# A graph-attention kernel: other superblock sizes at the end, a divided last quad, and ones written by ScalarE

## Chip, cores and metric

One NeuronCore of a Trainium2 chip runs the kernel. The metric is device time in microseconds (us) of one execution; of several runs the median is taken. The kernel before takes 2886.38 us (median of 5 runs, 2878.96 to 2889.55).

## What is computed

A graph with 12500 nodes and 200000 edges, sorted by destination. Each node's row `x` (128 numbers) is normalized and clipped at zero, and multiplied by a weight matrix; each edge gets an attention logit per head (4 heads) from its source, its destination and its 64 edge features. A softmax over all edges of one destination weighs the source rows, and the sum is added to `x`:

```python
h = jnp.maximum(_layernorm(x), 0.0)
h = (h @ W_node.T).reshape(N, H, HD)
e = (edge_attr_64 @ W_edge.T).reshape(E, H, HD)
att = jnp.sum(jnp.concatenate([h[src], h[tgt], e], -1) * a, axis=-1)
att = jnp.where(att > 0, att, 0.2 * att)
m = jnp.maximum(segment_max(att, tgt), 0.0)
ex = jnp.exp(att - m[tgt])
denom = segment_sum(ex, tgt) + (E - deg)[:, None] * jnp.exp(-m)
out = x + segment_sum((ex / denom[tgt])[:, :, None] * h[src], tgt)
```

## The kernel before

**Node part (lines 330 to 411).** A table of 137 numbers for each node is computed and written to device memory: four heads of 32 values with a one behind each, a further one for counting edges (column `R_CNT`), and four source logits (`R_SRC`).

**Edges.** They are cut into 392 groups of 511 edges (512 places); four groups are a *quad* (98 quads, numbered 0 to 97). GpSimd gathers the table rows of a quad's edges into a tile `ga` with 16 indirect DMAs (`gather`, line 135), 14 for the last quad. There are eight `ga` buffers, so the gather of quad q + 8 waits until quad q has been summed. The first four quads are gathered from `x`, before the table exists, and are turned into table rows on the chip by `converted` (lines 235 to 266): transposes and matmuls on TensorE, copies by ScalarE (line 261), and at the end of each quad two memsets by VectorE (lines 263 and 265) that put the ones in place. `late(q)` (line 709) runs it.

**Group loop (lines 775 to 807).** The quads are bundled in *superblocks*: 2 and 2 quads, then twenty-two of 4, then 2, 2, 1 and 1 (`ends`, line 426; 28 superblocks). For each quad there are two kinds of work, and for each superblock one:

- `logits(q)` (line 490): VectorE compares (line 497), TensorE multiplies (502, 505), and `add_sources` (517, 519) closes the quad. Opening a quad's logits also issues, on SyncE, the loads for the quad two ahead.
- `softmax(s)` (line 530): one chain across TensorE, VectorE and ScalarE for a whole superblock, from the transposes (544) through `low` (546), the scans (553, 575, 578, 581) and the exponential (587) to the copies `facs` (605) and `xs` (610).
- `sums(q)` (line 646): for each group, VectorE scales the gathered rows (663) and makes a one-hot matrix (666), and TensorE sums by matmul (671). `complete_group` (627) finishes the group before: VectorE carries the last row over (632), TensorE adds it (637), ScalarE copies the result to `pt` (638). After the fourth group ScalarE makes `den` (642), and one `complete` later VectorE divides the quad in six instructions (`divide`, 681 to 692). SyncE then stores the quad's four windows of `out` (694).

The order on every engine is that of the program: `together` takes one step of each of its generators in turn. The last quad of superblock s - 1 is summed together with the softmax of s and with the first logits of superblock s + 1; the other quads of s are summed together with further logits of s + 1, as long as there are any. So in this kernel a step of the loop is the sums of one quad with the logits of a later quad or without them, and with a softmax or without one.

Of the kernel before, what the change touches and what calls it, by code (L numbers as in the profile page):

```python
# [11 lines left out]
AF = mybir.ActivationFunctionType  # L12
OP = mybir.AluOpType
AX = mybir.AxisListType

P = 128
H, HD = 4, 32
HW = HD + 1
D = H * HD
# [5 lines left out]
R_CNT, R_SRC, ROW = H * HW, H * HW + 1, H * HW + 5  # L25

J = 4
GE = J * P
NE = GE - 1
WIN = 96  # L30
# [10 lines left out]
def blocks(total, step):  # L41
    return [(i, min(step, total - i)) for i in range(0, total, step)]
# [3 lines left out]
def kernel(  # L46
# [35 lines left out]
    nc = tc.nc  # L82
# [21 lines left out]
    ones = consts.tile([P, P], F32, name="ones")  # L104
# [13 lines left out]
    quads = blocks(G, QG)  # L118
    nq = len(quads)
# [26 lines left out]
    with tc.manual_schedule():  # L146
# [88 lines left out]
        def converted(q, psum, turn_pool, copy):  # L235

            ga = GA[q]
            m = quads[q][1]
            made = []

            def turned_over(i):
                hT_ps = psum.tile([P, 512], F32, name="acc")
                hT_ps = hT_ps.rearrange("p (j e) -> p j e", j=J)
                for j in range(J):
                    nc.tensor.transpose(hT_ps[:, j, :], ga[:, i, j, 0:D], ident)
                hT = turn_pool.tile([P, J, P], F32, name="hT_e", bufs=2)
                copy(hT, hT_ps)
                made.append(hT)

            turned_over(0)  # L250
            for i in range(m):
                yield
                if i + 1 < m:
                    turned_over(i + 1)
                for k in range(J // 2):
                    row_ps = psum.tile([P, 512], F32, name="acc")
                    row_ps = row_ps.rearrange("p (j e) -> p j e", j=2)
                    for j in range(2):
                        nc.tensor.matmul(row_ps[:, j, :ROW], made[i][:, 2 * k + j, :],
                                         wcat, start=True, stop=True)  # L260
                    nc.scalar.copy(ga[:, i, 2 * k:2 * k + 2, :], row_ps[:, :, :ROW])
            rows = ga[:, :m].rearrange("p g j r -> p (g j) r")
            nc.vector.memset(
                rows[:, :, 0:H * HW].rearrange("p t (h w) -> p t h w", w=HW)[:, :, :, HD], 1.0)
            nc.vector.memset(rows[:, :, R_CNT:R_CNT + 1], 1.0)
            yield


# [16 lines left out]
        with tc.tile_pool(name="node", bufs=2) as node, tc.tile_pool(  # L285
# [48 lines left out]
            ends = [3, 6]  # L334
# [88 lines left out]
    per = SBG // QG  # L423


    ends = [2, 2], [2, 2, 1, 1]
    amid = max(nq - sum(ends[0]) - sum(ends[1]), 0)
    supers = []
    for m in ends[0] + [n for _, n in blocks(amid, per)] + ends[1]:
# [5 lines left out]
    with tc.tile_pool(name="work", bufs=2) as work, \  # L435
            tc.tile_pool(name="turned", bufs=1) as turned, \
            tc.tile_pool(name="ps", bufs=1, space=bass.MemoryType.PSUM) as ps:
        XW, LG, AT, U, DR = {}, {}, {}, {}, {}
# [4 lines left out]
        share_ps = const_ps[0:WIN, WIN + G:].rearrange("p (g h) -> p g h", h=H)  # L443
# [10 lines left out]
        def window(g):  # L454
            return nc.values_load(
                base[0:1, g:g + 1], engines=[mybir.EngineType.SP], min_val=0, max_val=N - 1,
                skip_runtime_bounds_check_because="a destination, which is a node")
# [159 lines left out]
        state = {}  # L617

        def complete():

            division = state.pop("division", None)
            if begun:
                complete_group(*begun.pop())
            if division:
                divide(*division)

        def complete_group(q, i, ga, hot, pt, acc, fc):
            g0, m = quads[q]
            g = g0 + i
            if g:  # L630
                before = state["before"]
                nc.vector.tensor_tensor(  # L632
                    ga[0:1, i, 0, 0:H * HW].rearrange("p (h w) -> p h w", w=HW),
                    before[WIN:WIN + 1, 0:H * HW].rearrange("p (h w) -> p h w", w=HW),
                    fc.unsqueeze(2).to_broadcast([1, H, HW]), op=OP.mult)
                nc.scalar.copy(ga[0:1, i, 0, R_CNT:R_CNT + 1], before[WIN:WIN + 1, R_CNT:R_CNT + 1])  # L636
            nc.tensor.matmul(acc, hot[:, i, 0, :], ga[:, i, 0, :], start=False, stop=True)  # L637
            nc.scalar.copy(pt[:, i, :], acc)  # L638
            state["before"] = pt[:, i, :]
            if i == m - 1:  # L640
                den = work.tile([WIN, QG, H], F32, name="den")
                nc.scalar.activation(den[:, :m, :], pt[0:WIN, :m, R_SRC:R_SRC + H], AF.Exp,
                                     scale=-1.0)
                state["division"] = q, pt, den

        def sums(q):

# [25 lines left out]
                begun.append((q, i, ga, hot, pt, acc, fc[:, :, g - s0]))  # L673
                yield

        def divide(q, pt, den):

            g0, m = quads[q]
            xw = XW.pop(q)
            others = work.tile([WIN, QG], F32, name="others")  # L680
            nc.vector.tensor_scalar(others[:, :m], pt[0:WIN, :m, R_CNT], -1.0, float(E),
                                    op0=OP.mult, op1=OP.add)
            nc.vector.tensor_tensor(den[:, :m, :], den[:, :m, :],
                                    others[:, :m].unsqueeze(2).to_broadcast([WIN, m, H]), op=OP.mult)
            val = pt[0:WIN, :m, 0:H * HW].rearrange("p g (h w) -> p g h w", w=HW)
            nc.vector.tensor_tensor(den[:, :m, :], den[:, :m, :], val[:, :, :, HD], op=OP.add)
            nc.vector.reciprocal(share_ps[:, :m, :], den[:, :m, :])
            res = work.tile([WIN, QG, D], F32, name="res")
            nc.vector.tensor_tensor(  # L689
                res[:, :m, :].rearrange("p g (h d) -> p g h d", d=HD), val[:, :, :, 0:HD],  # L690
                share_ps[:, :m, :].unsqueeze(3).to_broadcast([WIN, m, H, HD]), op=OP.mult)
            nc.vector.tensor_tensor(res[:, :m, :], res[:, :m, :], xw[:, :m, 0:D], op=OP.add)  # L692
            for i in range(m):
                nc.sync.dma_start(out[bass.ds(window(g0 + i), WIN), :], res[:, i, :])

        def all_logits(q):
            flush()
# [11 lines left out]
        def late(q, copy=nc.scalar.copy):  # L709

            return [converted(q, acc_pool, work, copy)]
# [276 lines left out]
```

## Time and profile before

| what | value |
|---|---|
| median of 5 runs | 2886.38 us |
| the profiled execution's own time | 2883.8 us |
| its span, first to last instruction | 2881.9 us |
| TensorE matmul / VectorE / ScalarE / GpSimd busy | 48% / 47% / 15% / 52% of the span |
| mean granted TensorE clock | 0.522 |
| first gathers | 161 us |
| quad 0 summed (`den`, line 642) | 301.78 us |
| quad 97 summed | 2867.14 us |
| last store issued | 2876.27 us |

"Busy" counts computing instructions; waiting instructions and the issue of DMAs are not counted. In the rows of the profile, `out<-in` are tiles by the program's names, `x4` is a number of instructions, and the bracket of a timeline row gives the engine's idle time before it and what ended that. "issue" means that the profile shows nothing that was waited for, and "remote" that a semaphore was raised by something that the profile cannot name. One core runs here, so "remote" is no other core.

### The profile page before, as it was taken

The page shows a single profiled execution, that of the slowest core. Times are in us where ns is not written, and L with a number is a line of the kernel's source. Part 1 is how long each engine was busy: PE and PEld are TensorE (multiplying, and loading weights), DVE is VectorE, ACT ScalarE, POOL GpSimd, SP SyncE. Part 2 cuts the span into 40 slices and gives each one's busy share as a digit, 9 for nine tenths or more (in the row PEclk, how much of TensorE's full clock was granted, in tenths as well). Part 3 has the DMA queues.
Part 4 walks back from the last instruction along what each step waited for, and adds up shares of the span by engine and source line. Part 5 has one row for each costly group of instructions (what it writes and reads, how often), then busy time and mean ns, then how long its engine had stood idle before and what let it go on. Part 6 is the DMA issues. An engine that isn't in the chain of part 4 may idle for free.

```text
span 2881.9 us, 29033 instructions
## 1 busy us (share of the span) xinstructions
PE 1396.6 (48%) x7275; PEld 1253.9 (44%) x7275; DVE 1363.6 (47%) x3314; ACT 428.0 (15%) x1766; POOL 1491.8 (52%) x1574
## 2 busy tenths in 40 slices
PE   2524655445445455454454454454454454454465
PEld 1424644444444444444344444354454444444364
DVE  2523454444444454454454454354454454454376
ACT  1524201111111111111111111111111111111121
POOL 7152345555555555555556556555556555556510
PEclk6765555555555555555555555555555555555555
DMA  4333344343344344344344344344444343444320
GB/s 141 119 108 79 94 126 116 93 112 105 101 111 108 103 115 109 91 125 106 100 109 110 102 111 108 101 109 101 110 111 110 101 112 101 107 111 109 84 69 15
DMA packets 214493, 299.10 MB, mean 104 GB/s; under 512 B 86121, under 2 KB 162153, under 8 KB 204914
## 3 DMA queue, kind: packets, MB, share of 16 engines
q1 hardware_dynamic: 162512, 184.97, 23.2%
q0 software_dynamic: 50112, 109.65, 15.7%
q10 hardware_dynamic: 1698, 2.58, 0.3%
q8 instruction: 61, 1.00, 0.1%
q14 instruction: 110, 0.90, 0.1%
HBM read 270.49 MB, written 26.52 MB: 103 GB/s over the span
## 4 chain that ended last, share of the span: by engine, by line
another core or an unknown queue 23%; PE 15%; DVE 10%; issue 7%; ACT 2%; DMA 0%; SPq 0%; ACTq 0%; DVEq 0%
PE acc L671 8%; PE lg L505 3%; PE acc L637 2%; DVE at L497 2%; ACT pt L638 1%; DVE res L692 1%; DVE res L689 1%; DVE run L575 1%; DVE ga L632 1%; PE lg L502 1%; DVE hot L666 1%; DVE ga L663 1%; DVE run L553 0%; DVE top L581 0%
## 5 line engine op out<-in xcount | busy, mean ns | idle before, releaser
L135 POOL DMA_INDIRECT ga<-table,srci x1502 | 1430.1, 952 | 1241.2 <-PE acc L637 719.8
L671 PE MATMUL acc<-ga,hot 128*97 128x137 f32 x2352 | 650.6, 448 | 755.9 <-ACT ga L659 520.8
L671 PEld LDWEIGHTS acc<-ga,hot 128*97 128x97 f32 x2352 | 518.7, 279 | 782.5 <-ACT ga L659 530.1
L632 DVE TENSOR_TENSOR ga<-pt,facs 1x132 f32<-1x132 f32 x391 | 112.5, 288 | 1027.0 <-ACT pt L638 703.3
L638 ACT COPY pt<-acc 97x137 f32<-97x137 f32 x392 | 107.4, 274 | 2052.0 <-remote 1248.9
L505 PE MATMUL lg<-wblk,ea 128*128 128x8 f32 x1568 | 409.1, 359 | 0.0
L505 PEld LDWEIGHTS lg<-wblk,ea 128*128 128x128 f32 x1568 | 381.7, 309 | 0.0
L637 PE MATMUL acc<-ga,hot 128*97 128x137 f32 x784 | 263.0, 439 | 162.5 <-issue 76.1
L502 PEld LDWEIGHTS <-at 96*128 96x128 bf16 x1568 | 213.4, 165 | 226.8 <-DVE at L497 130.2
L663 DVE TENSOR_TENSOR ga<-ga,ex_ps 128x528 f32<-128x528 f32 x392 | 270.3, 690 | 8.6 <-PE ex_ps L598 8.2
L637 PEld LDWEIGHTS acc<-ga,hot 128*97 128x97 f32 x784 | 195.9, 282 | 178.2 <-issue 84.2
L497 DVE TENSOR_TENSOR at<-const_ps,db 96x512 bf16<-96x512 f32 x392 | 266.9, 682 | 7.4 <-DMA db<-in_dst_dram 1.5
L502 PE MATMUL lg<-pw,at 96*128 96x12 bf16 x1568 | 169.3, 181 | 154.5 <-DVE at L497 106.8
L666 DVE TENSOR_TENSOR hot<-const_ps,slot 128x384 f32<-128x384 f32 x392 | 213.8, 545 | 0.0
L598 PE MATMUL ex_ps<-ident,ex 64*128 64x64 f32 (+2 forms) x112 | 18.6, 314 | 212.1 <-ACT ex L587 212.1
L598 PEld LDWEIGHTS ex_ps<-ident,ex 64*128 64x128 f32 (+2 forms) x112 | 13.8, 208 | 215.1 <-ACT ex L587 215.1
L372 PE MATMUL row_ps<-wcat,hT 128*128 128x137 f32 x198 | 41.5, 362 | 83.7 <-DVE hT L364 24.9
L636 ACT COPY ga<-pt 1x1 f32<-1x1 f32 x391 | 73.9, 189 | 10.6
L372 PEld LDWEIGHTS row_ps<-wcat,hT 128*128 128x128 f32 x198 | 35.2, 254 | 90.0 <-issue 45.8
L135 POOL DMA_INDIRECT ga<-in_x_dram,srci x64 | 60.7, 948 | 20.7 <-issue 19.2
L692 DVE TENSOR_TENSOR res<-res,xw 96x512 f32<-96x512 f32 x98 | 67.8, 692 | 3.4
L689 DVE TENSOR_TENSOR res<-pt,const_ps 96x512 f32<-96x512 f32 x98 | 66.9, 683 | 3.4
(129 smaller groups left out, 1013.2 us busy)
## 6 DMA issues: line engine op xcount, KB each, us to landing
db<-in_dst_dram SPq DMA_DIRECT2D x98, 768.0 KB
ea<-in_edge_t_dram SPq DMA_DIRECT2D x98, 512.0 KB
ga<-table,srci POOLq DMA_INDIRECT x1502
xw<-in_x_dram SPq DMA_DIRECT2D x392, 48.0 KB
out_dram<-res SPq DMA_DIRECT2D x392, 48.0 KB
pw<-side SPq DMA_DIRECT2D x392, 2.2 KB
table<-row SPq DMA_DIRECT2D x9, 616.5 KB
xt<-in_x_dram SPq DMA_DIRECT2D x9, 576.0 KB
```

The source lines that it names most:

```text
L135: nc.gpsimd.indirect_dma_start(out=ga[:, i, j, 0:width], out_offset=None, in_=rows, in_offset=bass.IndirectOffsetOnAxis(ap=srci[:, g0 + i, ...
L497: nc.vector.tensor_tensor(at[:, i, :], node_ps[0:WIN, g0 + i:g0 + i + 1].to_broadcast([WIN, GE]), db[:, i, :], op=OP.is_equal)
L502: nc.tensor.matmul(lg[:, i, j].rearrange("p k h -> p (k h)"), at[:, i, j * P:(j + 1) * P], sw, start=i + j == 0, stop=False, skip_group_ch ...
L505: nc.tensor.matmul(lg[:, i, 2 * w:2 * w + 2, 0, :], ea[:, i, w, :], wblk, start=False, stop=True, skip_group_check=True)
L632: nc.vector.tensor_tensor(ga[0:1, i, 0, 0:H * HW].rearrange("p (h w) -> p h w", w=HW), before[WIN:WIN + 1, 0:H * HW].rearrange("p (h w) -> ...
L637: nc.tensor.matmul(acc, hot[:, i, 0, :], ga[:, i, 0, :], start=False, stop=True)
L638: nc.scalar.copy(pt[:, i, :], acc)
L663: nc.vector.tensor_tensor(val, val, heads(ex)[:, :, :, g - s0].unsqueeze(3).to_broadcast([P, J, H, HW]), op=OP.mult)
L666: nc.vector.tensor_tensor(hot[:, i, :, 0:WIN], lane_ps.unsqueeze(1).to_broadcast([P, J, WIN]), slot[:, g, :].unsqueeze(2).to_broadcast([P, ...
L671: nc.tensor.matmul(acc, hot[:, i, j, :], ga[:, i, j, :], start=j == 1, stop=False)
L689: nc.vector.tensor_tensor(res[:, :m, :].rearrange("p g (h d) -> p g h d", d=HD), val[:, :, :, 0:HD], share_ps[:, :m, :].unsqueeze(3).to_br ...
L692: nc.vector.tensor_tensor(res[:, :m, :], res[:, :m, :], xw[:, :m, 0:D], op=OP.add)
```

## The change

There are three edits.

1. The ones of the converted quads 0 to 3 are written by ScalarE, as two copies from a tile of ones, in place of the two memsets on VectorE.
2. The last superblocks have 3, 3, 2, 2, 2, 2 quads in place of 2, 2, 1, 1. The number of 4-quad superblocks falls from 22 to 20; there are 28 superblocks as before. Of the last 16 quads, those summed together with a softmax are 83, 86, 89, 91, 93 and 95, where they were 83, 87, 91, 93, 95 and 96; those summed without logits of a later quad are 82, 88, 95, 96 and 97, where they were 89, 90, 94, 96 and 97.
3. The last quad is divided and stored group by group: four times six VectorE instructions on one group each, and `den` is made four times by ScalarE.

TensorE, GpSimd and SyncE keep the number of their instructions. VectorE gets 18 more and loses 8, and handles smaller softmaxes at the end; ScalarE gets 11 more (8 copies and 3 `den`). The loop's waits in the 4-quad superblocks are the same as before.

```diff
             rows = ga[:, :m].rearrange("p g j r -> p (g j) r")
-            nc.vector.memset(
-                rows[:, :, 0:H * HW].rearrange("p t (h w) -> p t h w", w=HW)[:, :, :, HD], 1.0)
-            nc.vector.memset(rows[:, :, R_CNT:R_CNT + 1], 1.0)
+            nc.scalar.copy(
+                rows[:, :, 0:H * HW].rearrange("p t (h w) -> p t h w", w=HW)[:, :, :, HD],
+                ones[:, 0:1].unsqueeze(2).to_broadcast([P, m * J, H]))
+            nc.scalar.copy(rows[:, :, R_CNT], ones[:, 0:m * J])
...
-    ends = [2, 2], [2, 2, 1, 1]
+    ends = [2, 2], [3, 3, 2, 2, 2, 2]
...
-            if i == m - 1:
+            if i == m - 1 or q == nq - 1:
+                lo = i if q == nq - 1 else 0
                 den = work.tile([WIN, QG, H], F32, name="den")
-                nc.scalar.activation(den[:, :m, :], pt[0:WIN, :m, R_SRC:R_SRC + H], AF.Exp,
-                                     scale=-1.0)
-                state["division"] = q, pt, den
+                nc.scalar.activation(den[:, lo:i + 1, :], pt[0:WIN, lo:i + 1, R_SRC:R_SRC + H],
+                                     AF.Exp, scale=-1.0)
+                state["division"] = q, pt, den, lo, i + 1
...
-        def divide(q, pt, den):
+        def divide(q, pt, den, lo, hi):
+            n = hi - lo
+            xw = XW[q][:, lo:hi]
+            pt = pt[0:WIN, lo:hi]
+            den = den[:, lo:hi]
...
-            for i in range(m):
-                nc.sync.dma_start(out[bass.ds(window(g0 + i), WIN), :], res[:, i, :])
+            for i in range(n):
+                nc.sync.dma_start(out[bass.ds(window(quads[q][0] + lo + i), WIN), :], res[:, i, :])
```

More of the change, by code (lines that the diff above doesn't have):

```diff
@@ L674, in sums @@
                 yield
-        def divide(q, pt, den):
-            g0, m = quads[q]
-            xw = XW.pop(q)
+        def divide(q, pt, den, lo, hi):
[3 more added lines that the diff above has]
+            den = den[:, lo:hi]
             others = work.tile([WIN, QG], F32, name="others")
-            nc.vector.tensor_scalar(others[:, :m], pt[0:WIN, :m, R_CNT], -1.0, float(E),
+            nc.vector.tensor_scalar(others[:, :n], pt[:, :, R_CNT], -1.0, float(E),
                                     op0=OP.mult, op1=OP.add)
[L683 to L687, printed above, removed]
+            nc.vector.tensor_tensor(den, den, others[:, :n].unsqueeze(2).to_broadcast([WIN, n, H]),
+                                    op=OP.mult)
+            val = pt[:, :, 0:H * HW].rearrange("p g (h w) -> p g h w", w=HW)
+            nc.vector.tensor_tensor(den, den, val[:, :, :, HD], op=OP.add)
+            nc.vector.reciprocal(share_ps[:, :n, :], den)
             res = work.tile([WIN, QG, D], F32, name="res")
             nc.vector.tensor_tensor(
-                res[:, :m, :].rearrange("p g (h d) -> p g h d", d=HD), val[:, :, :, 0:HD],
-                share_ps[:, :m, :].unsqueeze(3).to_broadcast([WIN, m, H, HD]), op=OP.mult)
-            nc.vector.tensor_tensor(res[:, :m, :], res[:, :m, :], xw[:, :m, 0:D], op=OP.add)
-            for i in range(m):
-                nc.sync.dma_start(out[bass.ds(window(g0 + i), WIN), :], res[:, i, :])
+                res[:, :n, :].rearrange("p g (h d) -> p g h d", d=HD), val[:, :, :, 0:HD],
+                share_ps[:, :n, :].unsqueeze(3).to_broadcast([WIN, n, H, HD]), op=OP.mult)
+            nc.vector.tensor_tensor(res[:, :n, :], res[:, :n, :], xw, op=OP.add)
+            for i in range(n):
+                nc.sync.dma_start(out[bass.ds(window(quads[q][0] + lo + i), WIN), :], res[:, i, :])
         def all_logits(q):
```

## The prediction

> **What bounds the kernel now.** I read the busy shares first (no engine is over 52%, so none is simply full), then the waits, then the timelines of GpSimd and ScalarE against each other. Rows of the waits (engine, line, releaser: total us, times, longest):
>
> ```profile
> ACT pt L638 <- remote: 1248.9, 105, 18.9
> POOL ga L135 <- PE acc L637: 719.8, 86, 61.0
> ...
> DVE ga L263 <- issue: 39.8, 2, 21.1
> ```
>
> ScalarE waits about once in each of 98 quads, 1248.9 / 105 = 11.9 us each, for a sum that TensorE finished issuing long before; GpSimd waits for the last matmul of a quad (line 637), which frees a buffer. GpSimd's timeline:
>
> ```profile
> 2714.05 0.94 POOL L135 DMA_INDIRECT ga<-table,srci  x1 [5.12 <-PE acc L637]
> ...
> 2732.97 0.95 POOL L135 DMA_INDIRECT ga<-table,srci  x1 [0.30 <-issue]
> 2736.86 0.95 POOL L135 DMA_INDIRECT ga<-table,srci  x1 [2.94 <-remote]
> ```
>
> A batch of 16 gathers takes 2733.92 - 2714.05 = 19.9 us and starts when a quad is summed. The ends of quads, from ScalarE's timeline:
>
> ```profile
> 1501.52 0.22 ACT L642 ACTIVATE den<-pt 96x16 f32<-96x16 f32 x1
> 1524.67 0.22 ACT L642 ACTIVATE den<-pt 96x16 f32<-96x16 f32 x1
> 1550.56 0.22 ACT L642 ACTIVATE den<-pt 96x16 f32<-96x16 f32 x1
> 1576.30 0.22 ACT L642 ACTIVATE den<-pt 96x16 f32<-96x16 f32 x1
> 1608.66 0.22 ACT L642 ACTIVATE den<-pt 96x16 f32<-96x16 f32 x1
> ...
> 2776.74 0.22 ACT L642 ACTIVATE den<-pt 96x16 f32<-96x16 f32 x1
> 2789.51 0.22 ACT L642 ACTIVATE den<-pt 96x16 f32<-96x16 f32 x1
> 2809.75 0.22 ACT L642 ACTIVATE den<-pt 96x16 f32<-96x16 f32 x1
> 2820.46 0.22 ACT L642 ACTIVATE den<-pt 96x16 f32<-96x16 f32 x1
> 2840.14 0.22 ACT L642 ACTIVATE den<-pt 96x16 f32<-96x16 f32 x1
> 2857.81 0.22 ACT L642 ACTIVATE den<-pt 96x16 f32<-96x16 f32 x1
> 2867.14 0.22 ACT L642 ACTIVATE den<-pt 96x16 f32<-96x16 f32 x1
> ```
>
> While gathers run, a step with logits takes 25.8 us (1550.56 to 1576.30), one with a softmax too 32.4. After the last gather (2754.2) a step with logits takes 12.8 (2776.74 to 2789.51), with softmax and logits 20.2, with a softmax alone 17.7, of sums alone 9.3 to 10.7. So a gather batch holds the engines up: some 7 us of a step's work gets done beside its 20 us, the rest comes after it, and only then is the next buffer free. GpSimd and the compute engines take turns. The change leaves that loop alone from quad 4 to 81; it acts on three places at its ends.
>
> **Place 1, the ones (first edit).** VectorE's timeline:
>
> ```profile
> 260.86 0.17 DVE L201 SCALAR_TENSOR_TENSOR shift<-both,rstd 128x16 f32<-128x16 f32 x1
> 264.18 0.11 DVE L263 MEMSET ga<- 128x64 f32 x1 [3.14 <-ACT ga L261]
> ...
> 319.19 0.11 DVE L263 MEMSET ga<- 128x64 f32 x1 [18.68 <-issue]
> ...
> 323.04 0.27 DVE L519 TENSOR_TENSOR U<-st,ga 128x64 f32<-128x64 f32 x1
> 326.57 0.69 DVE L549 TENSOR_TENSOR t_ps<-t_ps,low 32x511 f32<-32x511 f32 x1
> ```
>
> The memset costs 0.11 us but waits for ScalarE's last copy, and everything behind it on VectorE waits too. Its four instances:
> - Quad 0 (236.5): behind it stands a copy that TensorE's transposes release only at 247.2. Nothing gained; ScalarE's two copies sit before row scalings that end 7 us earlier. 0.
> - Quad 1 (264.18): behind it stand 10 us of ready work (lines 517, 519, 497, 186), back to back until 271.0; ScalarE then waits for it (`rstd`, 271.04, idle 3.1 us). Without the memset VectorE goes on at 261.07 and is through at 267.9. ScalarE's own queue ends at 267.9 plus 0.4 for the two copies, so `rstd` moves from 271.04 to 268.3: **-2.7**.
> - Quad 2 (286.9): VectorE waited only 0.4 us; ScalarE is the late one (`facs` starts right as its scalings end, 287.83), so the two copies count: **+0.5**.
> - Quad 3 (319.19): TensorE and ScalarE convert until 318.67 + 0.39. VectorE can do lines 663, 666, the division of quad 0 and 517 meanwhile (3.3 us); `U` (519) needs the converted rows, so it moves from 323.04 to about 319.6. Next late is TensorE: sums (1.7 us), logits (1.1), transposes (0.9) from 319.8, then `low` 0.6: line 549 moves from 326.57 to about 324.1: **-2.4**.
>
> A ScalarE copy of these shapes isn't in the trace. From below: 0.12 us, the spacing of the 128x16 copies at line 659; from above: 0.39 us, line 261 with 128x274. I take 0.2 to 0.25, near 659's own 0.21. All eight on the path would cost 1 to 3 us. Sum -4.6; bounds -7 (3.14 and 3.9 gained in full) and +2 (the gathers of 301.7 to 321.2 still hold TensorE, and the copies cost).
>
> [...]
>
> **Place 2, the superblocks (second edit).** Number and kind of all work stay; only which step holds which changes.
> - Under gathers (quads 82 to 90): two steps with logits become a softmax step and the step after it. In the trace twenty 4-quad superblocks average 108.4 us (for example 1501.52 to 1608.66 is 107.1) against 4 x 25.8 = 103.1, so a softmax costs **+5.3** here, the following step giving back some 1.3 of 6.6. Two steps of sums alone stay two, 22.8 us each (last gather end + 2.7); the one with the short batch of 14 keeps its 2.5 us advantage.
> - After the gathers (91 to 97): softmax+logits three times, logits once, softmax once and sums twice before; now softmax+logits twice, logits twice, the rest alike: 12.8 - 20.0 = **-7.2**. A sums-only step after a softmax-only one took 9.3, another 10.7: I add 0.4.
>
> Sum **-1.5**; bounds -5 (the softmax is hidden under the batch as far as 7 us of compute are) and +4 (6.6 paid each time, sums 2 us dearer).
>
> **Place 3, the last quad (third edit).** Now: last `pt` at 2867.1, six divisions 2.4 us, then four stores, each waiting for the one before: 2869.55, 2872.16, 2874.75, 2876.27; the end follows 5.6 us later. A group's division, for which no row exists, is bounded by 2.4 (the whole quad) and 1.0 (six of the 0.17 us rows); from 0.17, 0.17, 0.18, 0.26 and two of 0.29 (1x132, line 632) with gaps I take 1.6. Divisions 0 and 1 stand before lines 663 and 632 on VectorE, so the last `pt` comes 1.6 us later, 2868.7; the last division ends at about 2870.9. The stores of quad 96 were issued from 2860.55 at 1.52 us spacing, the fourth at 2865.09; four more behind them at this spacing go at 2866.6, 2868.1, 2869.7 and 2871.2. Last store 5.1 us earlier; of its 7 gaps some will be slower (the median of this wait is 1.55, a tenth exceed 2.25, two of the last three were 2.60), so I take **-4.2**, bounds -5.5 and +2.5 (all at 2.60: 2860.55 + 18.2 = 2878.75). `res` has two buffers, so division 1 waits for quad 96's stores until about 2866.6, which fits.
>
> [...]
>
> **Sum.** -4.6 - 1.5 - 4.2 = **-10.3 us** on the profiled execution's 2883.8, so 2873.5; that one lies 2.6 below the median of the runs, 2886.4, so **2876.1**. About 0.2% (5.8 us) is what a measurement of this kernel can tell from no change.
>
> **Rivals.**
> - *VectorE wasn't what the start waited for* (chance 0.17): TensorE is still slowed by the gathers at 319 to 324 and by its own queue at 262 to 271. Place 1 is then 0, the rest -5.7: 2880.7, no change. For it: line 638 waits 11.9 us a quad beside gathers; against it: no gather runs from 242 to 301.
> - *The softmax moved under the gathers is paid in full* (0.11): place 2 at +4: -4.8, 2881.6. For it: 32.4 against 25.8; against it: 23.1 in the step after (1501.52 to 1524.67).
> - *Short superblocks starve beside gathers* (0.06, slower): where superblocks had two quads beside gathers, at the start, the steps of quads 1 and 2 took 41.2 and 35.5 us. If the three softmax steps at 83, 86 and 89 took their mean, 38.3, that is 6.0 more each, +18: 2894. It beats the gain from +3.4 a step. Against it: those early steps also held a conversion and two extra quads of logits.
> - The forecast as sized has the remaining 0.66.
>
> **How the numbers follow.** The forecast's cases lie beyond -5.8 nearly all, two rivals within: faster 0.66, same 0.27, slower 0.07. The bounds add to -17.5 and +8.5; together they are unlikely, so the range runs from 2867 (about -19 with a median's own scatter) to 2888, leaving out the starving case and little else.
>
> **What would show it.** Right: no VectorE instruction waits at 264 and 319; quad 0 is summed about 2.2 us earlier and quad 1 about 4.6; steps 83, 86, 89 at 32, 82 and 88 at 23, 96 at 9 to 10; last store about 4 us after the last `den`. Wrong: quad 1's end unmoved (place 1), steps 82 to 90 over 243 us in sum where 233.4 became 238.7 in my account (place 2), or store gaps over 2 us (place 3).

## The result, and the profile after

The changed kernel takes 2889.14 us (median of 41 runs, 2879.59 to 2898.89), the kernel before 2886.38 (70 runs, 2875.58 to 2897.24): 1.0012 times as long, 95% interval 1.0005 to 1.0019. The forecast was 2876.1, a gain of 10.3 us; measured is a loss of 2.8.

The profiled execution of the changed kernel took 2896.94 us (span 2895.2), 7.8 above its own median, and that of before 2.6 below its own. So the two profiled executions lie 13.1 us apart where the medians lie 2.8 apart: 10.4 us of what the profiles show between them is a difference of executions, not of kernels. By stage (when `den` of a quad is made, the end of its step):

| stage | before | after | difference | forecast |
|---|---|---|---|---|
| start to quad 0 | 301.78 | 299.22 | -2.6 | -2.2 (with the step of quad 1: -4.6) |
| step of quad 1 | 41.16 | 44.68 | +3.5 | -2.4 |
| quads 2 to 7 | 177.34 | 177.85 | +0.5 | 0 |
| quads 8 to 81 (unchanged code) | 2003.48 | 2017.25 | +13.8 | 0 |
| quads 82 to 90 (beside gathers) | 233.39 | 241.97 | +8.6 | +5.3 |
| quads 91 to 97 | 109.98 | 105.27 | -4.7 | -5.2 (-6.8, and 1.6 of edit 3) |
| last `den` to the end | 14.80 | 8.91 | -5.9 | -5.8 |

Quads 8 to 81 are where executions can differ so much: the 13.8 us lie in the 19 steps that follow a softmax (465.9 us before, 481.9 after; the 55 other steps give 2.2 back). These last 23.1 to 25.8 us each in either kernel. If the 10.4 us is put there, 13.8 - 10.4 = 3.4 us of the medians' difference remains in this part; that share is worked out, not seen.

**The start.** ScalarE's timeline of the kernel before, from the end of quad 0 to its last conversion copy (columns: start, duration, instruction, idle time before and what ended it):

```profile
301.78 0.22 ACT L642 ACTIVATE den<-pt 96x16 f32<-96x16 f32 x1
...
318.67 0.39 ACT L261 COPY ga<-acc 128x274 f32<-128x274 f32 x1 [2.42 <-remote]
```

The same of the changed kernel:

```profile
299.22 0.22 ACT L645 ACTIVATE den<-pt 96x16 f32<-96x16 f32 x1
...
311.20 0.39 ACT L261 COPY ga<-acc 128x274 f32<-128x274 f32 x1 [3.17 <-remote]
316.18 0.58 ACT L247 COPY hT_e<-acc 128x512 f32<-128x512 f32 x1 [4.59 <-remote]
...
321.76 0.97 ACT L261 COPY ga<-acc 128x274 f32<-128x274 f32 x3 [1.74 <-PE acc L259]
322.76 0.31 ACT L263 COPY ga<-ones 128x64 f32<-128x64 f32 x1
322.91 0.21 ACT L266 COPY ga<-ones 128x16 f32<-128x16 f32 x1
```

VectorE's timeline of the same stretch:

```profile
300.93 0.69 DVE L697 TENSOR_TENSOR res<-res,xw 96x512 f32<-96x512 f32 x1
301.53 0.35 DVE L518 TENSOR_REDUCE st<-lg 128x64 f32<-128x192 f32 x1
322.76 0.27 DVE L520 TENSOR_TENSOR U<-st,ga 128x64 f32<-128x64 f32 x1 [20.88 <-ACT ga L261]
...
327.54 0.69 DVE L550 TENSOR_TENSOR t_ps<-t_ps,low 32x511 f32<-32x511 f32 x1 [1.24 <-ACT low L547]
```

The memset's wait of 18.68 us is gone, and the division of quad 0 (down to line 697) is done at 301.6, 21 us earlier than before. But VectorE now waits 20.88 us one place further on, at `U`, for the same thing: the last converted rows. Those come at 322.73, 23.5 us after quad 0; before they came at 319.06, 17.3 us after it. Inside the gather batch ScalarE's longest waits are put down to "remote", and line 550 runs at 327.54 where the prediction had 324.1.

**Beside the last gathers.** ScalarE from quad 87 to 89:

```profile
2697.51 0.22 ACT L645 ACTIVATE den<-pt 96x16 f32<-96x16 f32 x1
...
2714.05 0.22 ACT L645 ACTIVATE den<-pt 96x16 f32<-96x16 f32 x1
2741.06 0.58 ACT L547 ACTIVATE low<-t_ps 32x511 f32<-32x511 f32 x1 [26.79 <-remote]
...
2758.05 0.22 ACT L645 ACTIVATE den<-pt 96x16 f32<-96x16 f32 x1
```

GpSimd's timeline there (the rows left out follow each other at 0.30 us):

```profile
2697.45 0.94 POOL L135 DMA_INDIRECT ga<-table,srci  x1 [3.18 <-remote]
...
2716.72 0.94 POOL L135 DMA_INDIRECT ga<-table,srci  x1 [0.30 <-issue]
2717.97 0.94 POOL L135 DMA_INDIRECT ga<-table,srci  x1 [0.30 <-issue]
...
2757.98 0.94 POOL L135 DMA_INDIRECT ga<-table,srci  x1 [20.36 <-PE acc L638]
```

Step 88, sums alone, ends at 2714.05: before its batch of gathers is over. Its buffer is free, so the next 16 gathers follow without a gap, 2697.45 to 2737.6. The softmax of step 89 is held through them: nothing of ScalarE's between 2714.3 and 2741.06, and nothing of VectorE's between 2717.4 and 2741.68. Then GpSimd has no free buffer and idles 20.36 us. Steps 88 and 89 take 16.54 + 44.00 = 60.5 us; the prediction had 23 and 32.

**The end** is as forecast: the last `den` is made at 2886.25, the last store issued at 2889.45, 3.2 us later (forecast: about 4). From the timelines of ScalarE and SyncE:

```profile
2886.25 0.20 ACT L645 ACTIVATE den<-pt 96x4 f32<-96x4 f32 x1
```

```profile
2889.45 0.32 SPq L699 DMA_DIRECT2D out_dram<-res  x1
```

### The profile page after: what moved, and what is told of

Same layout as the page of the kernel before. It is cut to its first block, busy times and chain, and to the rows that moved or that the text cites. A ratio compares the mean times of both kernels' runs of the same rounds, so it can differ in the third digit from the quotient of the medians.

```text
span 2895.2 us, 29065 instructions
## 1 busy us (share of the span) xinstructions
PE 1384.1 (48%) x7275; PEld 1252.4 (43%) x7275; DVE 1364.6 (47%) x3324; ACT 428.6 (15%) x1777; POOL 1489.6 (51%) x1574
## 3 DMA queue, kind: packets, MB, share of 16 engines
q1 hardware_dynamic: 162512, 184.97, 23.1%
## 4 chain that ended last, share of the span: by engine, by line
another core or an unknown queue 23%; PE 13%; DVE 9%; issue 6%; ACT 2%; DMA 1%; SPq 0%; ACTq 0%; DVEq 0%
PE acc L674 7%; PE lg L506 2%; PE acc L638 2%; DVE at L498 1%; DVE res L697 1%; DVE res L694 1%; ACT pt L639 1%; DVE run L576 1%; DVE ga L633 1%; DVE hot L669 1%; DMA out_dram<-res 1%; PE lg L503 1%; DVE ga L666 1%; DVE run L554 0%
## 5 line engine op out<-in xcount | busy, mean ns | idle before, releaser
L639 ACT COPY pt<-acc 97x137 f32<-97x137 f32 x392 | 107.1, 273 | 2047.6 <-remote 1301.0
L599 PEld LDWEIGHTS ex_ps<-ident,ex 64*128 64x128 f32 (+2 forms) x112 | 13.8, 207 | 207.0 <-ACT ex L588 207.0
L135 POOL DMA_INDIRECT ga<-in_x_dram,srci x64 | 60.5, 946 | 20.8 <-issue 19.2
L694 DVE TENSOR_TENSOR res<-pt,const_ps 96x512 f32<-96x512 f32 (+1 forms) x101 | 67.3, 667 | 5.4 <-DMA out_dram<-res 1.1
L697 DVE TENSOR_TENSOR res<-res,xw 96x512 f32<-96x512 f32 (+1 forms) x101 | 68.2, 675 | 3.5
```

The costliest lines, as they stand in the source:

```text
L135: nc.gpsimd.indirect_dma_start(out=ga[:, i, j, 0:width], out_offset=None, in_=rows, in_offset=bass.IndirectOffsetOnAxis(ap=srci[:, g0 + i, ...
L694: nc.vector.tensor_tensor(res[:, :n, :].rearrange("p g (h d) -> p g h d", d=HD), val[:, :, :, 0:HD], share_ps[:, :n, :].unsqueeze(3).to_br ...
L697: nc.vector.tensor_tensor(res[:, :n, :], res[:, :n, :], xw, op=OP.add)
```

## Experiments

**Theory.** Where gathers hold the other engines up (the *hold*, below), the change loses in two places: at quad 1 the conversion of quad 3 comes later than before, which takes back what the freed VectorE gains, and at quads 88 and 89 a short step lets two batches of gathers run into one. **Rivals:** ScalarE's copies cost more than the wait was worth; the new sizes cost by themselves; the loss is spread over the unchanged loop.

The runs came on chips of three kinds, told apart by the time of the kernel *before*: A, 2886 to 2888 us (the comparison above, and one run); B, 2072 to 2076 us (three chips, most runs); C, 2937 us. The granted clock doesn't tell them apart (0.522 to 0.540 in the profiled executions on A, 0.532 to 0.539 on B and C). What does: a register instruction of SyncE (columns: count, then duration in ns, least, median and most), in the changed kernel on A, in the kernel before on B, and in one of the kernels on C:

```profile
L699 SPq FUSED_REGOPS  x392: 3/37/709, 301.9 to 2888.0; - x196
```

```profile
L694 SPq FUSED_REGOPS  x392: 37/37/42, 166.5 to 2062.7; - x196
```

```profile
L698 SPq FUSED_REGOPS  x392: 2/37/716, 303.0 to 2918.1; - x196
```

This instruction takes up to 0.7 us on A and C, and at most 0.042 on B. A batch of 16 gathers takes 20 us on all three (19.9 in `before`, 19.7 in y2 and b1). And on B ScalarE's largest wait is for TensorE's work, not for "remote"; from the waits of the changed kernel on A, and of the kernel before on B:

```profile
ACT pt L639 <- remote: 1301.0, 105, 18.9
```

```profile
ACT pt L638 <- PE acc L637: 1290.1, 392, 14.9
...
POOL ga L135 <- issue: 465.5, 1527, 0.3
```

So B shows no hold: GpSimd issues its gathers one behind the other to the end (480 us idle in all, nearly all of it the 0.30 us in between). Its 1502 gathers from the table, at about 1.25 us each, are 1878 us of the 1911 from the first to the end of the last: their number sets the loop's time. Why chips differ in this can't be seen in these profiles and stays open.

| kernel | label | kind | median, us | before | ratio | 95% interval |
|---|---|---|---|---|---|---|
| edit 1 alone | e1_ones | B | 2065.83 | 2073.81 | 0.9958 | 0.9946 to 0.9971 |
| edit 2 alone | e2_super | B | 2063.97 | 2073.81 | 0.9953 | 0.9939 to 0.9967 |
| edit 3 alone | e3_last | B | 2069.53 | 2073.81 | 0.9978 | 0.9967 to 0.9989 |
| edit 1 without quad 3 | e4_ones012 | B | 2069.39 | 2073.81 | 0.9977 | 0.9967 to 0.9987 |
| edit 1, VectorE held | e5_hold | B | 2068.63 | 2074.83 | 0.9972 | 0.9957 to 0.9987 |
| e4 + edit 3, last superblock of 2 | e6_best | B | 2068.95 | 2074.83 | 0.9977 | 0.9967 to 0.9986 |
| whole change | a1_change | B | 2050.02 | 2072.34 | 0.9891 | 0.9878 to 0.9905 |
| whole change | c1_change | B | 2054.49 | 2076.06 | 0.9895 | 0.9878 to 0.9911 |
| change, last superblocks 2, 2, 2 | x1_222 | B | 2055.10 | 2073.16 | 0.9915 | 0.9901 to 0.9930 |
| the same | x2_222 | B | 2056.15 | 2076.06 | 0.9913 | 0.9896 to 0.9929 |
| the same | x3_222 | B | 2052.85 | 2072.75 | 0.9896 | 0.9876 to 0.9917 |
| e4 + edit 3, last superblocks 2, 2, 2 | y1_012_222 | C | 2923.50 | 2936.69 | 0.9956 | 0.9939 to 0.9972 |
| edits 2 and 3 | y2_no_ones | C | 2927.31 | 2936.69 | 0.9970 | 0.9958 to 0.9983 |
| edit 1 alone | y3_ones_again | C | 2932.23 | 2936.69 | 0.9985 | 0.9975 to 0.9994 |
| whole change | c2_change | A | 2894.03 | 2888.22 | 1.0016 | 0.9997 to 1.0035 |

Profiles of the kernel before were taken too: b1_before, b2_before and b3_before, all on B (2071.13, 2072.93 and 2071.68 us).

### The edits one by one, where nothing is held (B)

e1_ones, e2_super and e3_last each take one part of the diff; e4_ones012 keeps VectorE's memsets for the last converted quad:

```diff
+            if q == raw - 1:
+                nc.vector.memset(..., 1.0)
+            else:
+                nc.scalar.copy(..., ones...)
```

> The first edit alone: ScalarE writes the ones of quads 0 to 3, the rest as before. Theory A (the gathers hold the conversion of quad 3 longer once the work behind the memset, with its stores and loads, runs early): quad 0 is summed 2.5 us earlier than before (299.2), quad 1 about 1 us later (343.9), so +1 us in all, and nothing after quad 1 differs but by the scatter of single steps. Rival B (the eight ScalarE copies themselves are in the way): quad 0 not earlier, and the loss is spread over quads 2 and 3 in the length of the copies, 0.5 us each. Rival C (the edit shifts the phase of the whole loop): the steps after a softmax, 23 or 25.7 us, are more often 25.7, and the time is 5 us or more above before.

> The second edit alone: last superblocks of 3, 3, 2, 2, 2, 2 quads. Theory A (a step of sums alone beside gathers ends before its batch does, the next batch follows without a gap, and the softmax step is held through both): step 88 takes 16 to 17 us, step 89 about 44, the others as forecast; quads 82 to 97 together 2 us more than before's 343.4. Rival B (the two odd steps of the changed kernel were an accident of that execution): steps 88 and 89 at 23 and 32, quads 82 to 97 about 1.5 us less than before.

> The third edit alone: the last quad divided and stored group by group. Theory A: quad 97's sum ends 1.5 to 2 us later than before (a step of 11 us in place of 9.3), its last store 4 us or so earlier, the time 4 us less (ratio 0.9986); all steps up to quad 96 as before but for scatter. Rival B (the chain of stores of quads 96 and 97 fills what is gained): last store within 1 us of before.

> The first edit for quads 0 to 2 alone, quad 3's ones by VectorE as before. Theory A: quad 0 is summed 2.5 us earlier and quad 1 too, since the wait in front of quad 3's memset keeps the stores and loads behind it out of the gathers: step 1 at 41.2 as before, quad 1 ended at 340.4, time 2.5 us less (ratio 0.9991). Rival B (the copies are in the way): about as before. Rival C (step 1 is longer because its gathers start earlier relative to the loads of SyncE, whoever writes the ones): step 1 at 44 here too.

These expectations have numbers for A alone, the only kind that was known then. All four runs met B, so whether their theories A, B and C hold on A isn't shown by them.

Every edit gains: 8.0, 9.8 and 4.3 us, 22.1 in all, and the whole change on B measured 22.3 and 21.6. So no edit is a loss by itself, and they add up: the rivals of costly copies and of costly sizes are out for B. The profiles say where each gain lies. The time from the last gather to the end, 65.2 us in the kernel before (2004.1 to 2069.3), is 57.4 with edit 2, 61.0 with edit 3 and 53.1 with the whole change. Edit 1 works at the other end: quad 1's step is 26.8 us where it was 31.8 (31.1 and 31.0 in b2 and b3), and GpSimd's two long pauses for a buffer, 12.2 us, shrink to one of 4.6 (3.3 in the whole change, whose last gather ends at 1995.2). Over all profiles on B such pauses come to 9 to 15 us with quad 3's ones on VectorE, and to 1 to 5 with them on ScalarE (7.5 in e5, below). (At its far end the profile of e1 hardly shows the gain: its gathers were busy for 1447.7 us against 1441.3 in b1, and its last one ends 0.5 us earlier. That execution lies 5.5 us above its median.) Without quad 3's part (e4) the step is 31.7 again and 3.6 of the 8.0 us are gone.

### Which part of edit 1 counts (e5_hold, B)

Edit 1 with VectorE held back in the old place, by a copy that reads the last converted row:

```diff
+                if division[0] == 0:
+                    held = work.tile([P, 1], F32, name="held")
+                    nc.vector.tensor_copy(held, GA[raw - 1][:, QG - 1, J - 1, R_CNT:R_CNT + 1])
```

> The first edit alone, and in front of quad 0's division a copy of one column by VectorE that reads quad 3's last converted row: the division, quad 0's stores and SyncE's loads queued behind them wait for the conversion again, as behind the memset, while the two instructions ahead of the division (lines 663, 666) may run early. Where before takes about 2886 us: theory A (the stores and loads that come early are what holds the conversion longer) has step 1 back at 41 us and quad 1 ended 2 to 3 us before 342.9; rival B (the ScalarE copies, or the two early VectorE instructions) leaves step 1 at 44 to 45. Where before takes about 2074 us: step 1 was 31.7 us with the memset and 26.8 without it; all of theory A's gain there (5 us) goes with the wait, step 1 near 31.

VectorE's timeline around the division of quad 0, with the added copy (e5):

```profile
167.70 0.15 DVE L628 COPY held<-ga 128x1 f32<-128x1 f32 x1 [7.40 <-ACT ga L266]
...
170.38 0.27 DVE L520 TENSOR_TENSOR U<-st,ga 128x64 f32<-128x64 f32 x1
```

and without it (e1):

```profile
168.16 0.27 DVE L520 TENSOR_TENSOR U<-st,ga 128x64 f32<-128x64 f32 x1 [4.29 <-ACT ga L261]
```

In e1 `U` runs the moment the last rows are there; held back, it runs 2.7 us after the held copy. Quad 1's step is 29.95 us with this copy and 26.78 without, where the kernel before takes 31.0 to 31.8. So the wait ahead of the division is 3.2 of the 4.2 to 5.0 us that the edit saves in this step; the expectation had all of it. The rest, 1.0 to 1.8 us, this run doesn't explain. (The medians, 6.2 and 8.0 us gained, are from two chips, and their intervals overlap.)

### Other sizes, and the whole change (B)

The edit of x1, x2, x3 and y1 to the whole change; e6 has `[2, 2], [2]`:

```diff
-    ends = [2, 2], [3, 3, 2, 2, 2, 2]
+    ends = [2, 2], [2, 2, 2]
```

> Another plan from the same steps: superblocks of 2, 2, twenty-three of 4, and 2 (26 in place of 28, two softmaxes fewer, and no step of sums alone before the last gather), the third edit as in the change, the first for quads 0 to 2 alone. Where before takes about 2886 us, by the step times of its trace: quads 82 to 90 about 6 us more (three steps have logits that had none), quads 91 to 97 about 19 less, the last store 4 earlier, the start 2.5 earlier: 19 to 20 us less, ratio 0.993. Rival (with fewer superblocks the last softmax of four quads comes when nothing covers it): a gain of the third edit and the start alone, 6 us, 0.998. Where before takes about 2074 us: the same steps after the last gather, some 10 us less or more.

> The changed kernel, unchanged, in one call with the kernel before, to see what the change does on the chip at hand. Where before takes about 2886 us: steps 1, 88 and 89 again at 44 to 45, 16 to 17 and 44 us if they are no accident of the first profile (theory A), or at 41, 23 and 32 if they were (rival B); ratio 1.001. Where before takes about 2074 us, where no step is held by gathers and GpSimd issues them without a pause: the three edits alone gave 0.9958, 0.9953 and 0.9978 there; if they add up, 0.989 (23 us less); if the first edit's gain at the start is lost to the gathers, which end at the same time whatever the start does, the second and third alone, 0.993.

> The changed kernel with last superblocks of 2, 2, 2 quads in place of 3, 3, 2, 2, 2, 2 (27 superblocks in all): steps up to 90 are of the kinds that they were before the change, steps 91 to 97 of the kinds that they are after it. Where before takes about 2886 us: theory A (the superblocks lose because a step of sums alone beside gathers is followed by a softmax step) has steps 82 to 90 at 233 us as before and 91 to 97 at 105, the time 5 to 6 us below before although quad 3's conversion is still held longer; rival B (smaller superblocks at the end lose whatever stands before them) no better than the change. Where before takes about 2074 us: what is left after the last gather counts; if it is set by the last two superblocks alone, as the change, ratio 0.989; if by how early the superblocks get short, worse than the change by some 5 us.

> The whole change, on another chip. Theory: what it does depends on the chip. Where before takes about 2937 us, steps after a softmax last 25.9 us always, nothing can shift there, and the parts add (9.4 and 4.5): 13.9 less than before, about 2923, with the step of quad 89 near 29 us. Where before takes about 2886, it is 1 to 5 us slower again, most of it in steps after a softmax. Where before takes about 2073: 22 less. Rival (the parts disturb each other where gathers hold the engines up): 2933 or more on the 2937 chip, with a step of 44 us at quad 89 there too.

> The change with last superblocks of 2, 2 and 2 quads. Where before takes about 2937 us: like the kernel with quad 3's ones on VectorE (13.2 less), or 1 to 2 us better: 2922 to 2924, within 2 us of the whole change. Where before takes about 2886 us: if the step of 44 us belongs to the sizes and comes in every run, about 6 us under the whole change, 2881 to 2884; if it comes in single runs only, 2886 to 2889.

> The change with last superblocks of 2, 2 and 2 quads. Where before takes about 2886 us: no softmax follows a step of sums alone there beside gathers, so no step of 44 us; steps 88 and 89 lasted 60.5 and 60.8 us in the whole change where a step of sums and one of sums and softmax would take 23 and 29 to 32; so 6 to 8 us under the whole change, 2882 to 2885. Rival (the loss sits in the steady part): 2889 to 2893. Where before takes about 2937 us: 2922 to 2924. Where it takes about 2073: 17 to 20 less.

On B the sizes 2, 2, 2 may be a little worse than the change's own (0.9896 to 0.9915 against 0.9891 and 0.9895), but the intervals overlap. A single short superblock at the end (e6) is worth less: its two other parts alone multiply to 0.9977 x 0.9978 = 0.9955, and it measured 0.9977 (5.9 us, where some 10 were expected on B); 68.3 us are left after its last gather. No version beat the whole change on B. What x2 and x3 were to tell on A wasn't learned: they met B, so whether the sizes 2, 2, 2 avoid the loss on A is open.

> The kernel before, unchanged, for its profile on the chip at hand. Where it takes about 2074 us: step 1 near 31.7 us, GpSimd issuing without a pause over 10 us after quad 3, last gather issued near 2004 us and 65 to 66 us from there to the end. Where it takes about 2886 us: a second sample of the steps after a softmax (23 or 25.7 us), which tells how much of the difference between quads 7 and 81 is scatter: another sum by 5 us or more would say that it is.

> The kernel before, for a profile on the same chip. Where it takes about 2937 us, theory: quad 0 summed at 300.4, quad 1 at 345.9 to 346.7 (a step of 45.5 without ScalarE's ones too), all steps after a softmax at 25.9, steps 82 to 90 at 238 us in sum. Rival (ScalarE's ones of quad 3 lengthen the step of quad 1): that step at 41 to 42 us.

> The kernel before, for a profile. Where it takes about 2886 us, theory: quad 1's step at 41 us again and steps after a softmax between 23 and 26, 466 us for the 19 of them in the steady part; rival (the profile of before was one lucky execution): 44 to 45 us and 480. Where it takes about 2937: quad 1's step at 45.5, as without ScalarE's ones. Where it takes about 2073: as in the two profiles already there, 31 to 32.

### Where engines are held (C and A)

> All of the change, but with the ones of quad 3 by VectorE as before, and with last superblocks of 2, 2 and 2 quads. Where the kernel before takes about 2073 us, the gathers pace the loop and the parts add up: edit 1 without quad 3 is worth 4.4 us, the sizes 2, 2, 2 with edit 3 and all of edit 1 measured 18.1, so 14.5 less: 2058.6, slower than the whole change (2050.0). Where the kernel before takes about 2886 us, theory: the whole change loses 3.5 us in quad 1's step by quad 3's ones and about 5 us in the step of quad 89, where a softmax meets two gather batches without a gap; this kernel has neither, so 2879 to 2881, under before. Rival there (the loss is spread over the steady part and is in neither place): 2886 to 2890, like the whole change.

> The change without edit 1: superblocks and last quad only. Where before takes about 2073 us: the parts add (9.8 and 4.3), 14.1 less than before, 2059. Where before takes about 2886 us, theory: as the whole change within 1 us, for edit 1 gains 2.6 us at quad 0 and loses 3.5 in the step of quad 1; the loss at quad 89 stays: 2887 to 2889. Rival (edit 1 causes the drift of the steady part): 2880 to 2884.

> Edit 1 alone once more, on the chip of the two others. Where before takes about 2073 us: 8 less again, 2065 (it measured 2065.8 against 2073.8). Where before takes about 2886 us, theory: quad 0 is summed 2.6 us earlier and the step of quad 1 lasts 3.5 us longer, 2886 to 2888 in all; rival (edit 1 disturbs the steady part): 2890 and more, with quad 1 where theory has it.

> The whole change again, on another chip. Where before takes about 2937 us, theory: the parts add, 13.9 less, about 2923, the step of quad 89 near 29 us, steps after a softmax all at 25.9. Rival (the parts disturb each other): 2933 or more, with a step of 44 us at quad 89. Where before takes about 2886 us: 2887 to 2891 again. Where before takes about 2074: 22 less.

On C all parts gain: 13.2, 9.4 and 4.5 us. No kernel before had been met at 2937 us, so these three expectations have no number for it; for A, the other kind with a hold, their theory has a gain for y1 alone (5 to 7 us), and none for y2 and y3. So a hold alone doesn't make a loss, though the theory said that it would. The whole change was not run on C; if the parts add there as on B, it is 13.9 us ahead. On A its median came out 5.8 us behind, above the 2887 to 2891 that were expected, and the interval just takes in 1: no gain there either. The profiles of A and C differ in two places.

**Quad 1.** From y2 (ones on VectorE), ScalarE after the last converted row, and the same from y3 (ones on ScalarE):

```profile
321.89 0.22 ACT L659 CAST hot<-is_last 128x16 f32<-128x16 bf16 x1
321.99 0.57 ACT L661 COPY ga<-xs 128x16 f32<-128x16 f32 x4
328.89 0.58 ACT L546 ACTIVATE low<-t_ps 32x511 f32<-32x511 f32 x1 [6.32 <-PE t_ps L544]
```

```profile
323.34 0.31 ACT L263 COPY ga<-ones 128x64 f32<-128x64 f32 x1
...
327.51 0.58 ACT L547 ACTIVATE low<-t_ps 32x511 f32<-32x511 f32 x1 [3.23 <-PE t_ps L545]
```

Take the step apart at the end of the last conversion copy (line 261):

| kernel | kind, ones by | quad 0 to last conversion | from there to quad 1 | step |
|---|---|---|---|---|
| before | A, VectorE | 17.3 | 23.9 | 41.2 |
| after | A, ScalarE | 23.5 | 21.2 | 44.7 |
| c2_change | A, ScalarE | 23.5 | 21.2 | 44.7 |
| y2_no_ones | C, VectorE | 21.6 | 23.9 | 45.5 |
| y1_012_222 | C, VectorE | 22.4 | 23.9 | 46.3 |
| y3_ones_again | C, ScalarE | 24.1 | 21.2 | 45.3 |
| b1_before | B, VectorE | 7.9 | 23.9 | 31.8 |
| e1_ones | B, ScalarE | 6.9 | 19.9 | 26.8 |

The second part is 2.7 us shorter with edit 1 on A and on C, 4.0 on B: the gain is real, and its size that of the prediction. The first part is the one that the hold stretches: 7 to 8 us without it, 17 to 24 with it. With ScalarE's ones it is 1.7 to 2.5 us longer on C, which takes back most of the gain, and 6.2 on A, which turns it into a loss. On A the kernel before had this step in one profile only, as its three further profiles met B. That 17.3 is its rule is not shown, and with 21.6 and 22.4 on C it may be a lucky one. What makes the first part longer is argued only: in `after`, c2 and y3 the division is early, so SyncE issues quad 0's four stores and two loads at 303 to 312, inside the gather batch, and in `before`, y1 and y2 at 323 to 335, behind it.

**Quads 88 and 89.** ScalarE in c2 (A):

```profile
2719.58 0.22 ACT L645 ACTIVATE den<-pt 96x16 f32<-96x16 f32 x1
2746.74 0.58 ACT L547 ACTIVATE low<-t_ps 32x511 f32<-32x511 f32 x1 [26.94 <-remote]
...
2763.73 0.22 ACT L645 ACTIVATE den<-pt 96x16 f32<-96x16 f32 x1
```

and in y2 (C), which has the same superblocks:

```profile
2759.30 0.22 ACT L644 ACTIVATE den<-pt 96x16 f32<-96x16 f32 x1
2759.43 0.57 ACT L546 ACTIVATE low<-t_ps 32x511 f32<-32x511 f32 x1
...
2788.14 0.22 ACT L644 ACTIVATE den<-pt 96x16 f32<-96x16 f32 x1
```

Steps 87, 88 and 89 of `after`: 23.05, 16.54, 44.00; of c2: 23.09, 16.66, 44.15; of y2: 25.91, 23.26, 28.84. The step of 44 us is no accident of one execution: it came in both profiles on A, within 0.15 us. On C the fourth group of quad 88 gets through only after the batch (2759.00), GpSimd pauses 3.42 us for the buffer, and `low` runs at 2759.43, 0.2 us after the new batch begins, before that holds it up. The three steps cost 83.6 and 83.9 us on A against 78.0 on C. With this, steps 82 to 90 are worth +8.6 on A (+9.1 in c2) and 237.57 - 238.22 = -0.65 on C (y2 against y3, whose superblocks are those of before).

**The unchanged loop.** On C all steps after a softmax last 25.8 to 26.0 us, in all three kernels; on A they last 23.1 to 25.8, and come to 465.9 us for the 19 of them before, 481.9 and 480.9 in the two profiles of the change. Both these executions lie 7.8 and 7.9 us above their medians. That these steps vary on A within one execution is shown; that the change makes them longer isn't.

## Why the prediction was wrong, point by point

Two terms of the sum failed, quad 3's conversion (place 1) and the steps beside the last gathers (place 2); a third, the 0 for the unchanged loop, isn't settled.

- **What bounds the kernel:** right. Gathers hold the others up on that chip (in `before` a step with logits takes 25.8 us beside them and 12.8 after the last); on the chips that show no hold the same kernel takes 2072 to 2076 us.
- **Place 1, quads 0 to 2:** right as mechanism. `rstd` of quad 1 starts at 268.29 (forecast 268.3), quad 0 is summed 2.56 us earlier (forecast 2.2). From `rstd` of quad 0 to that of quad 1 it is 10.8 us in both profiles of A and C without ScalarE's ones (`before`, y2), and 7.95 in all four with them. In c2 quad 0 is summed at 301.19, so executions differ by 2 us there. The copies cost what was assumed: 0.31 and 0.21 us busy, and a pair moves what stands behind it by 0.4 us (from the last conversion copy's start to line 658 it is 0.68 us in y3, to the same instruction 0.28 in y2).
- **Place 1, quad 3 (-2.4): the step that failed first.** "Next late is TensorE ... from 319.8" took the end of the conversion from the trace of before as fixed. What follows it did become 2.7 us shorter; but the conversion itself runs inside a gather batch, and ended 23.5 us after quad 0 in place of 17.3. Quad 1 came 0.96 us later, not 4.6 earlier, close to the sign that the prediction set (its end unmoved). Why the conversion takes longer stays open. The rival "VectorE wasn't what the start waited for" had the right place (TensorE slowed beside the gathers), priced at 0; with quads 2 to 7 it is +1.5.
- **Place 2, beside gathers (+5.3): mechanism missed, +8.6.** The work was counted as a sum of steps of fixed length. The softmax steps 83 and 86 cost no more than priced (28.9 and 32.2), but "two steps of sums alone stay two, 22.8 us each" failed: in both profiles of A step 88, of sums alone behind a short step of 23.0 and 23.1, ended inside its own batch, two batches joined, and the softmax behind paid for both. (Behind a short step it needn't: in `before`, step 90 follows one of 22.8 and ended 2.9 us after its batch of 14.) Steps 88 and 89 are 5.5 us over the forecast; shorter steps elsewhere gave some back, so that the sum, 241.97, stayed under the 243 that the prediction had named as the sign. Step 89 is a starving softmax step as in the third rival, by another cause and in one place in place of three (44.0 where the rival had 38.3).
- **Place 2, after the gathers (-6.8):** -4.71 less the 1.76 by which edit 3 delays the last `den`: -6.5. Right.
- **Place 3 (-4.2):** 1.76 - 5.89 = -4.1. Right. The stores of the end go 1.5 us apart at first and up to 2.1 last; 1.52 was the row used.
- **"The change leaves that loop alone from quad 4 to 81":** the code, yes; the time, not shown. About 3.4 us of the medians' difference is left there.

The misses are 6.1 us up to quad 7 (+1.5 for -4.6), 3.3 beside the gathers, 3.4 in the loop and 0.4 in the last two places: 13.2, against 13.1 between forecast and measurement. That they agree is no check, since the third was got by subtraction. The first two rest on single executions: c2 has the same step of quad 1 (44.7) and the same steps 88 and 89, but at the end of quad 7 it is 6.3 us behind `before`, where `after` is 1.5 behind. The range failed with them: its upper end left out the starving case, and took the losses of several places as unlikely together, where both of those found arise inside gather batches.

## What to carry to other kernels

Where a transfer engine and the compute engines take turns, as on A here, a step has no length of its own: work that is freed earlier may only move into the held stretch (the division of quad 0 ran 21 us earlier, and VectorE then waited 20.88 us at `U`), and a step that ends inside its batch can let the next batch start at once, so that the step behind it pays for two (steps 88 and 89 of `after`: 16.54 and 44.00 us). Before short steps are put next to long ones there, find in the trace when each batch would start and which step would meet two of them. And time each part on the chip that counts: the same diff was worth -22 us on one kind of chip, about -14 by its parts on another, and +3 on the third.

## What the runs showed of the hardware

The same kernel takes 2073, 2886 or 2937 us on different chips, at the same granted clock (0.522 to 0.540 in the profiled executions on A, 0.532 to 0.539 on B and C) and with the same 20 us for a batch of 16 gathers. On the slower ones register instructions of SyncE last up to 0.7 us in place of 0.04, and the first gather from the table runs at 161 us in place of 92 to 96. While GpSimd issues gathers there, VectorE and ScalarE can stand still for long stretches (24 and 27 us, from 2714 to 2742 in `after`), and 1301.0 us of ScalarE's waits at the copy to `pt` (105 of them, in `after`) are put down to "remote", where in b1 all 392 of them are put down to TensorE. That chips differ in this was not foreseen, and the cause was not found.
